# First experts' tiles of a two-layer transformer: each pair of adapter merges ahead of a tile instead of behind it

## The chip, the cores and the metric

The program runs on one core of one Trainium2 chip. The time is device microseconds of one execution; the profile is one further execution of the same program. Engines are named as in the profile: PE is the matrix engine (PEld its weight loads), DVE the vector engine, ACT the scalar engine, POOL the GpSimd engine, and SP the engine that issues most of the transfers.

## The reference, cut to what matters

Four sublayers on 8 batches of 512 tokens with 512 features, each followed by a residual sum and a layer norm: a causal attention with 16 heads, a mixture of 8 experts, a second attention, and a quantised feed-forward layer. The mixture is the one that the change touches:

```python
router_logits = xf @ gate_weight.T + xf @ gate_delta.T
probs = softmax(router_logits)
routing_weights, selected = top_k(probs, 2)
gup = einsum('th,eho->teo', xf, gate_up_proj)
gup = gup + 2.0 * einsum('ter,eor->teo', einsum('th,erh->ter', xf, gup_lora_A), gup_lora_B)
gates, h = split(gup, 2)
h = silu(gates) * h
out = einsum('tei,eih->teh', h, down_proj)
out = out + 2.0 * einsum('ter,ehr->teh', einsum('tei,eri->ter', h, down_lora_A), down_lora_B)
y = sum over the two selected experts of out * routing_weights
x = layernorm(x + y)
```

Each expert has low-rank adapters of rank 16 for both of its matrices. The adapters' product depends on no token, so it can be added to the weights once.

## The kernel before

Only the two selected experts of a token are computed. A routing step writes each token into a table by expert, rows are gathered by that table into tiles of 128 tokens of one expert, and each tile goes through that expert's three products. The work on the first attention, the routing, the merging of adapters and the first tiles lies in one function, `attention0`. The order of PE's instructions there is the order in which the Python code makes them (`in_order(tc)`, entered at L1481); the orders of DVE, ACT, POOL and SP are made by a scheduler, which also picks the buffer that a tile of a pool gets.

**A tile** (`Tiles.step`, L938) puts on PE, in this order: half of the gate and up product of the next tile (two matmuls of 128x512 at L903), the two transposes of this tile's hidden rows (L911), the other half (L903), the product with the down matrix (two matmuls at L919), and four transposes that turn the rows of the tile three further on (L878). ACT and DVE make the activation (L904, L905), copy the transposed rows (L913, L879) and the result (L192 or L194); SP stores the result (L928), POOL issues the gather of a later tile's rows (L842). These have PSUM buffers of their own.

**A merge** (`merge`, L1404, which calls `Experts.merge`, L786) adds one of six slices of the adapters of a pair of experts to their weights. It makes two matmuls (L781), one for each expert of the pair; each has 16 rows and 512 columns, and the two lie in different groups of the array's rows. Each result stands in a buffer of the PSUM pool `a_mm` (tag `mm`), which has **two buffers** in all. ACT copies each out with a factor of 2 (L792, tile `scaled`), and POOL adds the copy to the weights (L794).

**Routing** shares those two buffers: the transposes of a batch's rows (`turn`, L1320, four buffers one after another), the router's logits (`score`, L491), their way back to tokens (`choose`, L503, read by DVE at L510 and L511), the ranks of tokens within experts (`dispatch`, L547 and L548, read by DVE at L554), one-hot rows made by DVE alone (`one_hot`, L577 to L579), and the table (`enter`, L588, sixteen matmuls of 128x256 in bf16, read by DVE at L589 and L590).

At the end of `attention0`, when the last batch's attention is done, the order is written out by hand. Of the 24 merges, 14 have been made by then. What follows alternates routing of the last two batches, tiles and merges: the table of the last batch but one (`enter`), two tiles each followed by a merge, `turn` of the last batch, a tile, `score`, a merge, `choose`, a tile, a merge, `dispatch`, two rounds of `one_hot`, tile and merge, the table of the last batch, and then tile and merge until no merge is left. These tiles are all of experts 0 to 3, while the merges are of experts 4 to 7. The result of a merge is wanted only by tiles behind this stretch.

The routing of the last batch is not wanted by these tiles either: their rows come from batches 0 to 5 (`t_soon`). Tiles further on take rows by the finished table (`t_fixed`).

Of the kernel before, what the change touches and what calls it, by code (L numbers as in the profile page):

```python
# [1213 lines left out]
def attention0(env, guard, keep, routes, experts, dram, p_mm, tiles_ctx):  # L1214
# [8 lines left out]
    with ExitStack() as phase:  # L1223
# [55 lines left out]
        def mm(shape, name):  # L1279
            return p_mm.tile(shape, F32, tag="mm", name=name)  # L1280
# [51 lines left out]
        def choose(b):  # L1332
            router.choose(b, logits.pop(b), mm([P, NT, E], "ps_r"))

        def dispatch(b):
            router.dispatch(b, mm([P, NT, E], "ps_rank"))
# [3 lines left out]
        def one_hot(b, places):  # L1340
            if places[0] == 0:
                rooms[b] = work.tile([P, ND, S], F32, tag="x1T", name="one_hot")
            return router.one_hot(b, rooms[b], places)

        def enter(rows):
            router.enter(mm([P, 2, E * E_TILES], "ps_table"), *rows)
# [57 lines left out]
        def merge(n=1):  # L1404
            for _ in range(min(n, len(merges))):
                e, c = merges.pop(0)
                ps = [mm([P, 512], "ps_lora") for _ in range(2)]
                experts.merge(e, c, ps, [work.tile([P, 512], F32, tag="r_inv", name="scaled", bufs=2) for _ in ps])
# [100 lines left out]
        project(b, 3)  # L1509
        experts.load(7)  # L1510
        enter(rows)
        for _ in range(2):
            tiles.step()
            merge()
        for c in range(ND):
            turn(b, c)
        tiles.step()
        score(b)
        merge()
        choose(b)  # L1520
        tiles.step()
        merge()
        dispatch(b)
        for places in ((0, 1), (2, 3)):
            rows = one_hot(b, places)
            tiles.step()
            merge()
        enter(rows)
        tiles.of_fixed = router.fixed(routes)
        while merges:  # L1530
            tiles.step()
            merge()
        order.close()
    return router, tiles, router.tables(routes, p_mm.tile([P, E], F32, tag="mm", name="ps_count"), guard.routed[:, 1:2])

# [289 lines left out]
def usual_pass(tc, ins, held_out):  # L1825
    nc = tc.nc
    with ExitStack() as ctx:
# [4 lines left out]
        with tc.tile_pool(name="a_mm", bufs=2, space=PSUM) as p_mm, ExitStack() as attn1_ctx:  # L1832
            with tc.tile_pool(name="routes", bufs=1, side="right") as routes, \
                    tc.tile_pool(name="experts", bufs=1, side="right") as pool, ExitStack() as tiles_ctx:
                experts = Experts(env, pool)
                router, tiles, tables = attention0(env, guard, keep, routes, experts, dram, p_mm, tiles_ctx)

                def load_rows(b):
                    rows = router.rows[S * b : S * (b + 1)]
                    nc.sync.dma_start(out=env.xs[b], in_=rows.rearrange("(t p) d -> p t d", p=P))  # L1840

                env.open_stream(ctx, range(2))
                rows = ctx.enter_context(tc.tile_pool(name="c_rows", bufs=1))
                own = attn1_ctx.enter_context(tc.tile_pool(name="c_own", bufs=1))
                attention = Attention1(env, guard, router, rows, own, p_mm, dram)
                beside = {tiles.next + 6 * (b + 1): lambda b=b: load_rows(b) for b in range(2)}

                for i, piece in enumerate(attention.first_pieces()):
                    beside[E * NT + 4 + 2 * i] = piece
                with in_order(tc, mybir.EngineType.DVE, mybir.EngineType.Activation, mybir.EngineType.Pool,  # L1850
                              mybir.EngineType.SP):
                    while tiles.next < tiles.n:
                        tiles.step()
                        next(tables, None)
                        beside.pop(tiles.next, lambda: None)()
                assert not beside and next(tables, None) is None
                tiles.rare()
# [314 lines left out]
```

## Time and profile before

| | |
|---|---|
| time, median of 3 runs (lowest, highest) | 2221.11 us (2220.45, 2225.37) |
| time of the profiled execution | 2228.55 us |
| its span, first to last instruction | 2226.8 us |
| mean granted TensorE clock over the span | 0.993 |
| PE busy | 2191.9 us, 98% of the span |
| first and last of the ten merges that the change moves, start | 773.10 and 849.53 us |
| POOL's addition of one expert's slice (L794), 48 times | median 1272 ns |
| ACT's copy of one expert's slice (L792), 48 times | median 597 ns |

In rows of the timeline the first column is the start in us from the span's start and the second the time to the end of the last instruction that the row merges; `xN` is the count. One fp32 matmul shows as two records. A bracket at the end of a row holds the idle time of the engine just before it and what ended it. In rows of windows the columns are the stretch, busy time and number of instructions of PE, PEld, DVE, ACT and POOL, then the granted clock of TensorE (1.00 is full speed), the share of the DMA engines and GB/s.

### The profile page before, as it was taken

To read this page: it belongs to the slowest core of one execution; us is meant where nothing else is said; L and a number is where in the kernel's file an instruction comes from. 1 tells how busy PE (TensorE), PEld (TensorE's weight loads), DVE (VectorE), ACT (ScalarE), POOL (GpSimd) and SP (SyncE) were. 2 spreads that over 40 slices of the span, in tenths; PEclk is the share of its full clock that TensorE was granted. 3 is DMA by queue.
4 is the path that set the end of the run, shared out by engine and by line. 5 is a ranking of instruction groups with operands and counts; after the bars stand their busy time and mean duration, and the time that the engine had idled before them with its cause. 6 is when DMAs were issued, how large, how long until landed. Compare 5 with 4: busy or idle time off the path is not lost. (4 is left out here: it accounts for less than half of the span.)

```text
span 2226.8 us, 23678 instructions
## 1 busy us (share of the span) xinstructions
PE 2191.9 (98%) x9006; PEld 1116.6 (50%) x9006; DVE 1273.7 (57%) x2032; ACT 632.0 (28%) x917; POOL 487.6 (22%) x489
## 2 busy tenths in 40 slices
PE   9999999999999999999999999999999999999997
PEld 3344444444444444444443333333343778888876
DVE  3556666666666633323316887798757655555443
ACT  2332323323233232122124333223332222222222
POOL 2322423234132333122105222222211000000000
PEclk9999999999999899999999999999999999999999
DMA  8010101101022216888735212312110321111000
GB/s 297 20 57 1 57 10 48 58 1 58 5 71 94 85 57 181 227 218 214 191 114 193 80 57 86 95 55 77 45 32 13 109 78 57 57 57 57 20 20 21
DMA packets 146428, 182.20 MB, mean 82 GB/s; under 512 B 60530, under 2 KB 89202, under 8 KB 144514
## 3 DMA queue, kind: packets, MB, share of 16 engines
q1 hardware_dynamic: 135024, 144.91, 21.0%
q0 software_dynamic: 10560, 34.61, 5.5%
q8 instruction: 74, 1.21, 0.2%
q10 hardware_dynamic: 722, 1.07, 0.1%
q14 instruction: 48, 0.39, 0.1%
HBM read 117.38 MB, written 63.18 MB: 81 GB/s over the span
## 5 line engine op out<-in xcount | busy, mean ns | idle before, releaser
L903 PE MATMUL ps_gu<-experts,xrT 128*128 128x512 f32 (+1 forms) x520 | 248.8, 601 | 0.0
L1360 ACT ACTIVATE p<-sc 128x2048 f32<-128x2048 f32 (+1 forms) x96 | 152.8, 1592 | 190.0 <-PE sc L1356 183.1
L1148 DVE SCALAR_TENSOR_TENSOR hT<-ps_u,vec,sg 128x512 f32<-128x512 f32 x88 | 65.6, 745 | 195.2 <-PE ps_u L1143 195.2
L1365 POOL TENSOR_SCALAR_AFFINE_SELECT p<-p 128x512 f32<-128x512 f32 x128 | 91.6, 729 | 385.2 <-ACT p L1360 378.5
L1159 PE MATMUL ps_f<-ffn_w,h_half 128*128 128x512 f32 x672 | 170.2, 394 | 0.6 <-issue 0.4
L998 POOL TENSOR_TENSOR g_total<-g_total,r_inv 128x512 f32<-128x512 f32 x64 | 89.7, 1401 | 358.3 <-DVE r_inv L1735 283.0
L1705 ACT ACTIVATE p<-sc 128x1024 f32<-128x1024 f32 x128 | 124.0, 1021 | 105.9 <-PE sc L1702 100.8
L1735 DVE RECIPROCAL r_inv<-r_inv 128x512 f32<-128x512 f32 x32 | 107.1, 3346 | 78.8 <-ACT r_inv L995 78.8
L1388 DVE TENSOR_TENSOR p<-p 128x1536 f32<-128x1536 f32 (+2 forms) x96 | 129.4, 1348 | 39.2 <-POOL p L1365 22.2
L905 DVE TENSOR_TENSOR h<-ps_gu,h 128x256 f32<-128x256 f32 x67 | 28.4, 424 | 212.8 <-ACT h L904 212.8
L903 PEld LDWEIGHTS ps_gu<-experts,xrT 128*128 128x128 f32 x520 | 96.2, 197 | 89.7 <-issue 89.5
L1159 PEld LDWEIGHTS ps_f<-ffn_w,h_half 128*128 128x128 f32 x672 | 124.4, 188 | 33.0 <-DVE h_half L1154 5.6
L1143 PE MATMUL ps_g<-x_high,ffn_w 128*128 128x512 f32 x352 | 138.9, 395 | 0.8 <-DVE x L1676 0.8
L1143 PE MATMUL ps_g<-x_low,ffn_w 128*128 128x512 f32 x352 | 139.1, 395 | 0.0
L1143 PE MATMUL ps_u<-x_low,ffn_w 128*128 128x512 f32 x352 | 138.8, 394 | 0.0
L1143 PE MATMUL ps_u<-x_high,ffn_w 128*128 128x512 f32 x352 | 138.7, 394 | 0.0
L919 PE MATMUL ps_y<-experts,hT 128*128 128x512 f32 (+1 forms) x272 | 127.9, 593 | 0.5 <-ACT hT L913 0.5
L1702 PE MATMUL sc<-qT,kT 64*128 64x512 f32 x512 | 127.3, 615 | 1.0 <-ACT qT L1609 0.7
L1292 PE MATMUL ps_q<-experts 128*128 128x512 f32 x256 | 121.1, 615 | 4.4 <-DMA experts<-in_xT 4.4
L1724 PE MATMUL av<-p,v 128*64 128x512 f32 x512 | 123.8, 605 | 0.0
L1285 PE MATMUL ps_v<-experts 128*128 128x512 f32 x256 | 118.0, 609 | 3.3 <-DVE v L1287 3.3
L1670 PE MATMUL ps_o<-attn_out,aoT 128*128 128x512 f32 x256 | 117.9, 605 | 0.8 <-ACT r_inv L995 0.8
(262 smaller groups left out, 3438.5 us busy)
## 6 DMA issues: line engine op xcount, KB each, us to landing
results<-y SPq DMA_DIRECT2D x68, 256.0 KB, 2.3
turned<-turned SPq DMA_DIRECT2D x56, 256.0 KB, 4.1
pair<-xrT SPq DMA_DIRECT2D x25, 512.0 KB, 3.4
xrT<-pair SPq DMA_DIRECT2D x100, 128.0 KB, 4.5
x<-in_x SPq DMA_DIRECT2D x8, 1024.0 KB, 7.5
experts<-in_gate_up SPq DMA_DIRECT2D x8, 1024.0 KB, 10.8
rows<-x SPq DMA_DIRECT2D x32, 256.0 KB, 2.0
x<-rows SPq DMA_DIRECT2D x8, 1024.0 KB, 15.5
```

The source lines that it names most:

```text
L903: nc.tensor.matmul(ps, lhsT=xT[:, c, :], rhs=self.weights(i, c), start=c == 0, stop=c == ND - 1)
L919: self.nc.tensor.matmul(ps, lhsT=hT[:, c, :], rhs=self.weights(i, ND + c), start=c == 0, stop=c == self.NI - 1)
L1143: nc.tensor.matmul(ps, lhsT=w[:, ts(dc, P)], rhs=x[:, dc, :], start=(dc, i) == (0, 0), stop=(dc, i) == (ND - 1, 1))
L1159: self.nc.tensor.matmul(os[t], lhsT=h[:, ts(t, P)], rhs=self.weights(2 * NHID + c), start=(c, i) == (0, 0), stop=(c, i) == (NHID - 1, 1))
L1285: nc.tensor.matmul(ps, lhsT=xts[b][:, c, ts(t, P)], rhs=wv[:, c, :], start=c == 0, stop=c == ND - 1)
L1292: nc.tensor.matmul(ps, lhsT=wq[:, g, ts(c, P)], rhs=xts[b][:, c, :], start=c == 0, stop=c == ND - 1)
L1360: nc.scalar.activation(p, sc[:, :, :width], AF.Exp, scale=scale)
L1388: nc.vector.tensor_tensor(total[:, :, P * kt :], total[:, :, P * kt :], p[:, :, at : at + w], ALU.add)
L1670: nc.tensor.matmul(ps, lhsT=state[b]["aoT"][:, c, ts(t, P)], rhs=w_out[:, c, :], start=c == 0, stop=c == ND - 1)
L1702: nc.tensor.matmul(sc[:, j, :], lhsT=st["kT"][hs, ts(kt, P)], rhs=st["qT"][g][hs, :], start=True, stop=True)
L1705: nc.scalar.activation(p, sc, AF.Exp, scale=scale)
L1724: nc.tensor.matmul(st["av"][HD * j : HD * (j + 1), :], lhsT=st["v"][:, kt, HD * j : HD * (j + 1)], rhs=p[:, j, :], start=kt == 0, stop=kt ...
```

## The change

Every merge of the stretch that stood directly behind a tile is called directly ahead of it. The matmuls, copies and additions stay the same in number and size, and so do the tiles and the routing steps; what changes is what lies next to what. Seen from routing: the table of the last batch but one is now followed by a merge, then a tile; `turn`, `dispatch` and the last batch's table now follow a tile instead of a merge; `choose` and `dispatch` and that table are now followed by a merge; `score`, merge, `choose` and merge stand in one row.

```diff
         enter(rows)
+
         for _ in range(2):
+            merge()
             tiles.step()
-            merge()
         for c in range(ND):
             turn(b, c)
         tiles.step()
         score(b)
         merge()
         choose(b)
+        merge()
         tiles.step()
-        merge()
         dispatch(b)
         for places in ((0, 1), (2, 3)):
             rows = one_hot(b, places)
+            merge()
             tiles.step()
-            merge()
         enter(rows)
         tiles.of_fixed = router.fixed(routes)
         while merges:
+            merge()
             tiles.step()
-            merge()
         order.close()
```

In the program built from it the instructions of all engines are the same in kind and number. The buffers of `a_mm` that the scheduler picks, called 0 and 1 here, are these (before, then after), in PE's order from the first table on; a bar is a tile, and M is a merge's pair:

```
before  table 1 | M 0,1 | M 0,1  turn 0,1,0,1 | logits 0  M 1,0  r 1 | M 0,1  rank 0 | M 1,0 | M 1,0  table 1 | M 0,1 | M 0,1 | M 0,1 | M 0,1
after   table 1  M 0,0 | M 1,0 | turn 1,0,0,1 | logits 0  M 1,0  r 1  M 0,1 | rank 0  M 1,1 | M 0,1 | table 0  M 1,0 | M 1,0 | M 1,0 | M 1,0 |
```

Behind the stretch the buffers of `a_mm` alternate in both programs, with 0 and 1 exchanged.

## The prediction

> **What bounds the kernel now.** I read the page first, for the engine that is never idle:
>
> ```profile
> span 2226.8 us, 23678 instructions
> ...
> PE 2191.9 (98%) x9006; PEld 1116.6 (50%) x9006; DVE 1273.7 (57%) x2032; ACT 632.0 (28%) x917; POOL 487.6 (22%) x489
> ...
> PEclk9999999999999899999999999999999999999999
> ```
>
> PE is busy for 98% of the span, and no other engine for more than 57%. A microsecond that PE loses in the stretch of the change is therefore lost at the end as well, unless a later wait takes it up, and behind the stretch hardly any are left. The last row says that the granted clock dips in one slice of 55.7 us, the one from 779 us on, which is the stretch of the change. The second view is PE's waits from 760 to 852 us, all of them:
>
> ```profile
> PE ps_x1T L1320 <- ACT scaled L792: 0.7, 1, 0.7
> PE ps_rank L547 <- ACT scaled L792: 0.7, 1, 0.7
> PE ps_table L588 <- ACT scaled L792: 0.7, 1, 0.7
> PE ps_x1T L1320 <- DVE x1T L194: 0.3, 1, 0.3
> ```
>
> Each of the first three is a routing step that wants one of the two buffers of `a_mm` straight after a merge took both, so it waits until ACT has copied one out. These are the waits that a tile in between would hide. The third view is the timeline, here of a tile between two merges and of the `turn` behind the second, and, from earlier, of how long a buffer is held:
>
> ```profile
> 738.85 0.60 ACT L792 ACTIVATE scaled<-ps_lora 128x512 f32<-128x512 f32 x1 [2.16 <-PE ps_lora L781]
> 739.49 0.29 PEld L781 LDWEIGHTS ps_lora<-lora 16*128 16x128 f32 x2 [0.44 <-ACT scaled L792]
> ...
> 767.20 1.88 PE L903 MATMUL ps_gu<-experts,first_turned 128*128 128x512 f32 x4
> ...
> 773.10 1.13 PE L781 MATMUL ps_lora<-lora 16*128 16x512 f32 x4
> 774.16 1.98 PE L903 MATMUL ps_gu<-experts,xrT 128*128 128x512 f32 x4
> ...
> 780.16 1.13 PE L781 MATMUL ps_lora<-lora 16*128 16x512 f32 x4
> 782.03 1.15 PE L1320 MATMUL ps_x1T<-ident,x 128*128 128x128 f32 x8 [0.74 <-ACT scaled L792]
> ```
>
> A tile takes PE 5.90 us (767.20 to 773.10) and a merge's pair 1.06 us (773.10 to 774.16); its two matmuls lie in different rows of the array and run beside each other. The first two rows belong to two merges in a row: a matmul of a merge that began at 737.63 was copied from 738.85 to 739.45, and the next user of its buffer began at 739.49. **A buffer is held for 1.86 us from the matmul's start.** The last view is the granted clock in six stretches of 3.41 us, which is the step in which it changes:
>
> ```profile
> 781.29:784.70 3.41, 2.37 (x18) 1.96 (x18) 1.23 (x2) 1.77 (x4) 2.70 (x3) 1.00 0.49 156
> 791.53:794.94 3.41, 3.41 (x14) 1.74 (x14) 0.38 (x2) 2.72 (x4) 1.83 (x3) 1.00 0.44 141
> 794.94:798.36 3.42, 3.42 (x7) 1.60 (x6) 2.55 (x17) 1.35 (x4) 0.74 (x1) 0.50 0.00 0
> 801.77:805.18 3.41, 2.67 (x12) 1.36 (x12) 1.83 (x7) 1.08 (x2) 1.53 (x2) 1.00 0.21 77
> 805.18:808.60 3.42, 3.42 (x7) 1.38 (x6) 3.35 (x19) 0.37 (x1) 0.96 (x1) 0.50 0.00 0
> 818.84:822.25 3.41, 2.67 (x20) 1.77 (x20) 0.95 (x2) 1.08 (x2) 1.53 (x2) 1.00 0.20 77
> ```
>
> The clock is halved behind the second and the fourth of them, and not behind the first and the last. What tells them apart is how full the array was: time of streaming, times the share of its rows and columns in use. A merge's pair is four records of 0.43 us on 16 of 128 rows, 0.21 us. From 801.77 that is 0.21 for the merge, some 0.05 for the ranks and 1.09 of the tile from 804.09 on: 1.35 of 3.41, a fill of 0.40. From 791.53 it is 0.30. From 818.84 it is 0.21 for the merge and 1.53 of table, 0.51; from 781.29 it is 0.59. A fill of up to 0.40 was followed by half the clock, one of 0.51 was not. A tile that meets a halved window took 7.68 us (794.08 to 801.76, and 804.09 to 811.77 again), so a window costs 7.68 - 5.95 = 1.73 us; 5.95 lies between the tiles of 5.90 and, from 812.83, 6.00 us.
>
> **The change part by part.** Nothing is added or removed in number; what changes is which wait stands where. The buffers are those that the built program names.
>
> *`turn`* follows a tile. Before, merge, wait and transposes took 780.16 to 784.40, 4.24 us. The wait of 0.74 goes. But its third buffer is now that of the second chunk, which ACT copied out 1.77 us after the first transpose (783.21 + 0.59 against 782.03), where before the third began 1.44 us after it: transposes 2.37 + 0.38 = 2.75. With the merge, 1.06 + 2.75 = 3.81: **-0.43**.
>
> *The first table* is followed by a merge whose two matmuls both get buffer 0, since buffer 1 holds the table until DVE has read it, and DVE is then behind four layer-norm rows until 771.5. The second matmul waits for the copy of the first: 1.86, and then its own 0.86 (two records of 0.43), 2.72 us against 1.06: **+1.66**. At most it takes a pair's 1.06, and the term is 1.86. ACT has been idle there for 19 us, so the copy is not late. Behind the waiting matmul PE's whole queue stands.
>
> *`choose` and the merge behind it.* In the trace L503 gives way to the tile at 794.08. The first new matmul goes then; the second wants the buffer of `choose`, which DVE's L511 frees at 794.68, so it runs to 794.72 + 0.86 = 795.58: 1.50 against 1.06, **+0.44**. If DVE is late, this grows with it.
>
> *`dispatch`* loses its wait (801.76 to 803.62 was 1.86 for merge and wait; 1.06 remains, **-0.80**), but the merge behind it gets buffer 1 twice, **+1.66** as above.
>
> *The last table* loses its wait (818.83 to 820.70, 1.87; **-0.81**). The merge behind it uses both buffers, and the second is free when DVE has read the table: L590 ended at 823.52, 1.08 us after the table gave way at 822.44. So 1.08 + 0.04 + 0.86 = 1.98 against 1.06: **+0.92**. The remaining merges lie between tiles as before.
>
> What moves along costs nothing while its cover holds. POOL's additions (1.27 us each) stand in another order to the gathers (0.95 us), which serve a tile three further on, 17 us or more; SP's load of the next attention's weights (1536 KB, at 853.94) passes one result store, whose buffer is wanted again two tiles, 12 us, later. Without this cover each would cost its own length once.
>
> The sum without the clock: -0.43 + 1.66 + 0.44 - 0.80 + 1.66 - 0.81 + 0.92 = **+2.64 us**.
>
> *The clock.* The steps of 3.41 us lie at random to the program. One falls to 0.40 or less when it holds at most 1.37 us of work, so some 1.15 of tile beside a merge and 2.25 of an almost empty stretch. A stretch of length L then catches one with a chance of about (L - 1.1)/3.41. Before: merge, wait and `choose` (791.30 to 794.08, 2.8) 0.5, merge and ranks (2.33) 0.36; the profiled execution had both. After: table's merge (2.72) 0.48; both merges around `choose` (791.30 to 795.58, 4.3) 0.94; ranks and merge (0.47 + 2.72 = 3.2) 0.62. That is 2.0 against 0.86, and a halved window makes the rest of an empty stretch longer, so that a second follows more easily. I take **two more windows, +3.46**, between one (1.73) and three (5.19).
>
> The Trainium skill, page "TensorE: Matmul & The Clock Gate", section "Why this matters for your kernels", asks only that no idle gap between bursts be longer than about 3 us. The longest gap that I add is 1.0 us, so by that rule no window is added and the sum is +2.6 us. The rows above speak against it: the window from 791.53, after which the clock is halved, has PE busy in all its 3.41 us.
>
> **The sum.** +2.64 + 3.46 = +6.1 us. The profiled execution took 2228.55 us, 7.4 more than the median of the runs, with the clock halved in seven steps of 3.41 us up to 810 us; on it the sum gives 2234.7, and on the median, which I forecast, **2227.2 us**.
>
> **The rivals.**
>
> *No more halved windows (2223.8 us).* Only the +2.64 remain. For it: the first of the three new places catches a window only every other time. Against it: the stretch around `choose` is longer than a step. 0.22.
>
> *The windows vanish (2220.3, not slower).* The place is `dispatch` and `choose`: a tile now lies between the merge and the ranks, and if both windows of before go and none comes, 2.64 - 3.46 = -0.8. It decides where every empty stretch is under 2.25 us; the doubled buffers speak against it. 0.06.
>
> *The change does what it says (2218.9, not slower).* The three waits go, -2.2, and the doubled buffers cost nothing because the second matmul could go elsewhere. The built program speaks against it. 0.07.
>
> *DVE is held up by POOL (2229.7).* The merge behind `choose` brings two additions of 1.27 us beside DVE's chain of small steps (795.46 to 799.40). At 804.40 and 805.22 two steps of 0.18 us took 0.56 and 0.97, while POOL added. The ranks wait for the chain; PE comes to them at about 801.5, so the chain has 2 us of cover, and what exceeds it, at most the 2.5 us of both additions, is added to my sum. 0.13.
>
> **How the numbers follow.** My forecast has 0.52, with 2225.5 to 2228.9 as its own range (one to three windows). A measurement here tells 0.2%, 4.4 us, from no change, so "slower" begins at 2225.55. It takes nearly all of the forecast (0.48), the last rival (0.13) and the upper edge of the first (0.04): 0.65. "Faster" needs less than 2216.7, 0.02. The rest, 0.33, is no change. The range goes from 2222.5, below the first rival by one window's share of the runs' spread, to 2231.5, the last rival with another window.
>
> **What would show it.** Right: PE's waits name `scaled` in front of L781 twice, about 1.0 us each, none of the three old waits is left, and the granted clock is halved three to five times between 763 and 825 us. Wrong: both matmuls of the merges behind the first table and behind the ranks start together, or the halved steps there stay at two or fewer. If the ranks wait for DVE, the last rival has its place.

## The result, and the profile after

| | before | after |
|---|---|---|
| time, median (lowest to highest; runs) | 2223.61 us (2220.45 to 2226.35; 8) | 2231.10 us (2227.98 to 2232.48; 8) |
| time of the profiled execution | 2228.55 us | 2231.41 us |
| its span | 2226.8 us | 2229.6 us |

The ratio of after to before is 1.0036, with a 95% interval of 1.0026 to 1.0045: the changed kernel is 7.5 us slower. The forecast was 2227.2 us, +6.1 us on a median of 2221.11. The direction was right and the time lies in the range of 2222.5 to 2231.5, but the size is off by 3.9 us.

The three rows of the page of after that answer to those of before:

```profile
span 2229.6 us, 23679 instructions
...
PE 2194.0 (98%) x9006; PEld 1116.6 (50%) x9006; DVE 1278.5 (57%) x2032; ACT 633.2 (28%) x917; POOL 488.5 (22%) x489
...
PEclk9999999999999899999999999999999999999999
```

PE still bounds everything. These totals hardly show the loss, since a matmul at half the clock counts as busy. Nor does the last row: its one dip, here the slice from 724.6 to 780.4 us, comes from four halved steps between 722 and 746 us, ahead of the stretch, and before has four there too. PE's waits in after, from 760 to 870 us, all of them:

```profile
PE ps_lora L781 <- ACT scaled L792: 1.5, 2, 0.7
PE ps_x1T L1320 <- ACT x1T L192: 0.7, 1, 0.7
```

The three waits of 0.7 us on `scaled` in front of `turn`, the ranks and the table are gone, as the change has it. In their place stand two of the same length in front of a merge's second matmul, where both matmuls of a merge got the same buffer (a doubled buffer, in what follows), and one inside the transposes. No wait on DVE is left or added. In the timeline of after:

```profile
765.51 1.12 PE L781 MATMUL ps_lora<-lora 16*128 16x512 f32 x2
767.38 1.12 PE L781 MATMUL ps_lora<-lora 16*128 16x512 f32 x2 [0.75 <-ACT scaled L792]
768.43 1.98 PE L903 MATMUL ps_gu<-experts,first_turned 128*128 128x512 f32 x4
...
781.40 1.04 PE L1320 MATMUL ps_x1T<-ident,x 128*128 128x128 f32 x8
783.12 1.09 PE L1320 MATMUL ps_x1T<-ident,x 128*128 128x128 f32 x8 [0.68 <-ACT x1T L192]
784.05 1.88 PE L903 MATMUL ps_gu<-experts,xrT 128*128 128x512 f32 x4
...
824.25 2.17 PE L781 MATMUL ps_lora<-lora 16*128 16x512 f32 x4
826.35 1.99 PE L903 MATMUL ps_gu<-experts,xrT 128*128 128x512 f32 x4
```

The first merge is torn apart, into two rows of two records: the second matmul begins 1.87 us after the first, and the tile begins 2.92 us after the merge, where a pair takes 1.06. The transposes take 784.05 - 781.40 = 2.65 us. The merge behind the last table takes 826.35 - 824.25 = 2.10. Then the granted clock in after, in some of the steps of 3.41 us in which it changes:

```profile
766.50:769.91 3.41, 2.66 (x7) 1.06 (x7) 2.91 (x4) 1.20 (x2) 2.38 (x3) 1.00 0.73 276
...
790.40:793.81 3.41, 3.41 (x21) 1.56 (x13) 0.35 (x1) 2.04 (x4) 1.81 (x2) 1.00 0.48 154
793.81:797.22 3.41, 3.41 (x6) 1.48 (x6) 2.25 (x10) 2.45 (x4) 2.09 (x3) 0.50 0.02 5
797.22:800.63 3.41, 3.41 (x7) 1.52 (x6) 3.24 (x13) 0.00 (x0) 1.91 (x2) 0.50 0.00 0
804.05:807.46 3.41, 2.66 (x13) 1.36 (x11) 3.25 (x13) 0.60 (x1) 0.70 (x1) 1.00 0.21 77
807.46:810.87 3.41, 3.41 (x5) 1.26 (x5) 3.38 (x12) 0.60 (x1) 1.83 (x2) 0.50 0.00 0
```

Three steps are at half the clock, two behind `score`, merge, `choose` and merge, and one behind the ranks and their merge. PE is busy in all of 790.40 to 793.81, and the clock is halved all the same; from 766.50, where it is idle for 0.75 us, it is not.

To compare executions I take the stretch from the first table's first matmul (L588) to `ps_count` (L623), which holds the same work in both kernels. In the profiled execution of before it took 91.05 us with two halved steps, in that of after 95.59 with three.

### The profile page after: what moved, and what is told of

It is laid out like the page before. It is cut to its first block, busy times and chain, and to the rows that moved or that the text cites. A ratio compares the mean times of both kernels' runs of the same rounds, so it can differ in the third digit from the quotient of the medians.

```text
span 2229.6 us, 23679 instructions
## 1 busy us (share of the span) xinstructions
PE 2194.0 (98%) x9006; PEld 1116.6 (50%) x9006; DVE 1278.5 (57%) x2032; ACT 633.2 (28%) x917; POOL 488.5 (22%) x489
```

## The experiments

The theory after the result: the loss has two parts, the merges whose second matmul waits for the copy of the first, and halved clock steps, which follow a step in which the array had too little work. By this theory the number of halved steps differs from execution to execution, since the steps of 3.41 us lie at random to the program, and that is also where before's own scatter comes from. The rivals: that idle time, not little work, brings the half clock; and that the clock plays no part in the difference at all.

**Both kernels again.** Neither is edited; each gives another profile.

> The kernel before once more, for its own number of halved clock steps. Theory: an execution's time is a base of 2216.4 us (2228.55 less seven halved steps of 1.73 us each) plus 1.73 us for each halved step that falls ahead of 850 us, and an execution at the median (2223.6) has about four of them; so this profile lies on that line within 1 us, and the two or three that the first profile had in the stretch from 763 to 850 us need not be there. Rival: the first profile lay 5 us above the median for another reason; then a profile near 2224 us shows seven halved steps as well.

> The changed kernel once more. Theory: base 2219.3 us (2231.41 less seven halved steps of 1.73), 2.9 us above the base of before, and three to five halved steps in the stretch from 763 to 850 us; the profile lies on that line within 1 us, the ratio to before is 1.003 to 1.0045. Rival (the loss is in the waits alone, the clock plays no part in the difference): as many halved steps as before's second profile in the stretch, and a time that does not follow their number.

Measured: 2224.91 us for before (11 runs, ratio 1.0004, 0.9993 to 1.0014) and 2231.27 us for after (7 runs, ratio 1.0033, 1.0021 to 1.0044). The stretch of each, as windows, first before and then after:

```profile
762.23:849.90 87.67, 85.15 (x308) 41.11 (x306) 34.03 (x102) 26.98 (x54) 35.96 (x32) 1.00 0.28 93
```

```profile
765.12:862.77 97.65, 95.48 (x307) 44.79 (x306) 37.08 (x102) 27.34 (x54) 36.08 (x32) 0.93 0.28 97
```

In this execution of before the stretch has no halved step and takes 3.38 us less than in the first, which had two: **1.69 us for a halved step**. The execution of after has four. The line that was expected of whole executions, a base and 1.73 us for each halved step, was a rough one: before's second lies 1.5 us below the 2216.4 + 4 x 1.73 that it should have had, after's second 0.2 below its own.

**A third profile of each**, to see whether the stretch keeps to a line.

> The kernel before, a third profile. Theory: from the first table's start to ps_count 87.67 us + 1.7 us for each halved step there (none, one or two), within 0.3 us. Rival (something else than the clock varies between executions): more than 0.5 us off that line.

> The changed kernel, a third profile. Theory: from the first table's start to ps_count 87.67 + 2.9 = 90.6 us + 1.7 us for each halved step there, of which there are two to four, within 0.5 us. Rival (something else than the clock varies between executions): more than 1 us off that line.

Measured: before 764.00 to 855.05, 91.05 us with two halved steps, the same to the hundredth as the first. After 763.30 to 860.92, 97.62 us with four, on its line within 0.3 us. In before nothing but the clock varies in the stretch; in after the three profiles, less 1.69 us for each halved step, agree to 0.4 us.

**Fuller matmuls.** This one tells the rivals apart: the same waits and buffers, but more of the array in use. It is a probe of time only: the five merges that it widens do not compute the product of one expert's adapters.

> As the changed kernel, but the matmuls of five merges, those next to routing, use all 128 rows of the array instead of 16, with zeros between the adapters; the product then holds the adapters of four experts and not of one. Where the second matmul of a merge waits for the copy of the first, this costs nothing (the first runs 0.86 of the 1.86 us either way); around score and choose some 0.5 us in all. Waits and buffers stay. Theory (a step of 3.41 us is followed by half the clock when the array was filled to 0.40 or less): the stretch from 763 to 850 us has no halved step or one, and the time is 2231.1 - 4 x 1.73 + 0.5 = about 2224.7 (2222.5 to 2227.5). Rival (the waits, that is PE's idle time, bring the half clock): three to five halved steps as in the changed kernel and 2231 to 2232. Rival (the clock plays no part in the difference): 2231 to 2232 too, whatever the number of halved steps.

```diff
+        i and self.nc.gpsimd.memset(self.lora, 0.0)
...
-    def delta(self, ps, e, c):
+    def delta(self, ps, e, c, wide):
         j = 32 * (e % 4)
-        a, bt = lora_factors(self.lora[j : j + R, :], c)
+        a, bt = lora_factors(self.lora if wide else self.lora[j : j + R, :], c)
...
-                experts.merge(e, c, ps, [...])
+                experts.merge(e, c, ps, [...], len(merges) in (9, 7, 6, 5, 3))
```

Measured: 2225.57 us (11 runs, ratio to before 1.0005, 0.9996 to 1.0015), 5.7 us less than the changed kernel in the same series. Its waits of PE are the very two rows shown for after. Its merge behind the ranks, and its clock in the steps around `choose` and the ranks and over the stretch:

```profile
800.51 1.10 PE L781 MATMUL ps_lora<-lora 128*128 128x512 f32 x2
802.36 1.13 PE L781 MATMUL ps_lora<-lora 128*128 128x512 f32 x2 [0.75 <-ACT scaled L792]
803.32 1.88 PE L903 MATMUL ps_gu<-experts,xrT 128*128 128x512 f32 x4
```

```profile
789.79:793.20 3.41, 3.41 (x18) 1.82 (x14) 0.38 (x2) 2.54 (x4) 1.80 (x3) 1.00 0.48 154
793.20:796.62 3.42, 3.42 (x11) 1.69 (x10) 2.45 (x6) 1.99 (x5) 3.03 (x3) 1.00 0.02 5
800.03:803.45 3.42, 2.67 (x12) 1.37 (x11) 3.39 (x13) 0.60 (x1) 1.06 (x1) 1.00 0.20 77
803.45:806.86 3.41, 3.41 (x11) 1.57 (x10) 3.38 (x14) 0.97 (x2) 1.46 (x2) 1.00 0.00 0
...
762.86:852.85 89.99, 87.70 (x308) 42.75 (x307) 36.73 (x102) 27.29 (x54) 36.47 (x32) 1.00 0.30 105
```

No step is halved, though PE is busy for the same 2.67 of 3.42 us around the ranks as it was in after (2.66 of 3.41), where half the clock followed. The share of the array that works, counted as in the last section, is 0.60 in that step and was 0.19 in after. Idle time is the same, work is more: it is the work that counts. Both rivals, which wanted 2231 to 2232 us, fall.

**Parts of the change alone.** First the first loop alone, then `choose`'s merge alone, then all but the first loop.

> The kernel before with only the first loop's two merges ahead of their tiles. Buffers there are as in the changed kernel (both matmuls of the merge behind the table in buffer 0), everything behind the transposes as before. Theory (the doubled buffer costs 2.92 - 1.06 = +1.86 as seen in the changed kernel's profile, the transposes' wait gives -0.5, and the emptier stretch catches a halved step in some half of the executions, +0.8): before + 2.2 us, 2226.6 (2225.2 to 2228). Rival (merges lie as well here as there, the loss is around choose and the ranks alone): 2223.5 to 2224.5.

```diff
         for _ in range(2):
+            merge()
             tiles.step()
-            merge()
```

Measured: 2228.67 us (11 runs, ratio 1.0015, 1.0005 to 1.0025), +3.3 us by the ratio and 0.7 us above the range that I gave. The stretch takes 94.17 us with three halved steps, one of them new, at 767.76, behind the torn merge. Without them it is 1.43 us above before's; +1.86 for the merge and -0.5 for the transposes would be +1.36. The rival falls.

> The kernel before with only choose's merge ahead of its tile, so that score, merge, choose and merge stand in one row and the ranks follow a tile. Theory: +0.44 for the merge, -0.80 for the ranks' wait; the row of 4.3 us nearly always catches a halved step where before two places caught 0.3 of one each, +0.7: before + 0.3, 2224.7 (2223.5 to 2226); its profile shows one or two halved steps around choose and none at the ranks. Rival (DVE's chain is held up by POOL's two additions): the ranks wait for DVE and the time is over 2226.

```diff
         choose(b)
+        merge()
         tiles.step()
-        merge()
```

Measured: 2223.88 us (11 runs, ratio 1.0001, 0.9992 to 1.0010), no change that the runs can tell, and within the range that I gave. The stretch takes 89.04 us with one halved step, behind `choose`'s merge. In its waits of PE only the transposes and the table are left; the ranks wait for nobody:

```profile
PE ps_x1T L1320 <- ACT scaled L792: 0.7, 1, 0.7
PE ps_table L588 <- ACT scaled L792: 0.7, 1, 0.7
PE ps_x1T L1320 <- DVE x1T L194: 0.3, 1, 0.3
```

So POOL's two additions beside DVE's chain do not reach PE. Without its halved step the stretch is 87.35 us, 0.3 below before's: with -0.80 for the wait, +0.48 is left for the merge and the small steps around it.

> The changed kernel with the first loop's two merges back behind their tiles; the ranks' merge still has both matmuls in buffer 1. Theory: from the first table's start to ps_count, PE takes 87.67 us (the second profile of before, which had no halved step there) + 1.7 (0.4 for choose's merge, -0.8 and -0.8 for two waits, 1.86 and 1.04 for the merges behind the ranks and the last table) = 89.4 us, and 1.7 us more for each halved step, of which one to three are expected; the time is before + 4 us (2226.5 to 2229.5), and this gain over the changed kernel, 3 us, is what first_table lost. Rival (the two halves are not additive, since a halved step in the first half moves the phase of the second): over 2230, or under 2226.

```diff
         for _ in range(2):
-            merge()
             tiles.step()
+            merge()
```

Measured: 2228.87 us (12 runs, ratio 1.0020, 1.0011 to 1.0029); the stretch takes 94.18 us with three halved steps, 89.11 without them, where 89.4 was expected. The excesses add up, as far as intervals of 0.1% either way can tell: 0.15% for the first loop and 0.20% for the rest, against 0.33 to 0.36% for the whole.

**Merges inside tiles.** A merge directly ahead of a routing step made that step wait (before); one directly behind the first table or the ranks got a doubled buffer (after). Two versions put merges elsewhere.

> Merges neither behind a tile nor ahead of it but inside, between the tile's gate and up product and its product with the down matrix, so that no merge's buffer is wanted by the next routing step and no merge directly follows one. The merge between score and choose stays. Theory: the three waits of before go (-2.3 us), no merge waits for a copy, and the almost empty stretches are shorter than the 2.25 us that a halved step needs, but for score, merge and choose: at most one or two halved steps in the stretch. 2223.6 - 2.3 - 1.7 = about 2219.6 (2217.5 to 2221.5), faster than both kernels. Rival (the change's loss is not from where merges lie but from the tiles that come later): no better than before, 2223 to 2226. Rival (a merge inside a tile holds up the tile's own chain on ACT): waits of PE for hT or for ps_y's copy appear and the time is over 2224.

```diff
-    def step(self):
+    def step(self, middle=lambda: None):
...
+        middle()
         self.down(i)
...
-            tiles.step()
-            merge()
+            tiles.step(merge)
...
```

The same is done at all four places where a merge stood behind a tile. Measured: 2221.91 us (11 runs, ratio to before 0.9989, 0.9980 to 0.9998), 0.4 us outside the range that I gave. The expectation had missed one thing: the buffers of the transposes become 0, 1, 1, 0, and so one wait of 0.7 us on ACT's own copy stays. It is the only wait of PE in the stretch, which takes 88.01 us with one halved step, behind `score`, merge and `choose`.

> As the kernel with merges inside tiles, but one tile of the first loop goes between score and choose, and the tile behind the transposes takes a merge too: no routing step has a merge or another routing step beside it. Theory: the three waits and the 0.81 us between score's merge and choose go, -2.4 to -3.1, and no almost empty stretch is longer than 1.1 us, so no halved step falls between 763 and 850 us in its profile: before - 2.6 - 1.0 = 2220.8 (2218.8 to 2222), faster than both kernels and than the one with merges inside tiles by about 1 us. Rival (routing steps want tiles behind them for DVE's sake, and moving the transposes one tile forward makes them wait for the layer norm): PE waits for x at the transposes and the time is 2223 or more.

```diff
         enter(rows)
-        for _ in range(2):
-            tiles.step(merge)
+        tiles.step(merge)
         for c in range(ND):
             turn(b, c)
-        tiles.step()
+        tiles.step(merge)
         score(b)
-        merge()
+        tiles.step(merge)
         choose(b)
         tiles.step(merge)
```

The diff is against the version before it. Measured: 2220.58 us (11 runs, 2217.89 to 2222.47; ratio to before 0.9984, 0.9975 to 0.9993), as expected and **faster than both kernels**, before by 0.16%. The rival would have had the transposes wait for the layer norm; PE's waits are one row, on DVE's copy of an earlier chunk. That row, and the stretch:

```profile
PE ps_x1T L1321 <- DVE x1T L194: 0.5, 1, 0.5
```

```profile
763.52:849.06 85.54, 85.03 (x307) 40.10 (x306) 32.99 (x102) 26.98 (x54) 36.15 (x32) 1.00 0.28 98
```

**All profiled executions together.** The halved steps are those within the stretch; "full clock" is the stretch less 1.69 us for each; "outside" is the execution's time less the stretch.

| execution | time | stretch | halved | full clock | outside |
|---|---|---|---|---|---|
| before, first | 2228.55 | 91.05 | 2 | 87.67 | 2137.5 |
| before, second | 2221.80 | 87.67 | 0 | 87.67 | 2134.1 |
| before, third | 2226.92 | 91.05 | 2 | 87.67 | 2135.9 |
| after, first | 2231.41 | 95.59 | 3 | 90.52 | 2135.8 |
| after, second | 2234.64 | 97.65 | 4 | 90.89 | 2137.0 |
| after, third | 2232.63 | 97.62 | 4 | 90.86 | 2135.0 |
| fuller matmuls | 2224.59 | 89.99 | 0 | 89.99 | 2134.6 |
| first loop alone | 2228.97 | 94.17 | 3 | 89.10 | 2134.8 |
| `choose`'s merge alone | 2226.80 | 89.04 | 1 | 87.35 | 2137.8 |
| all but the first loop | 2227.31 | 94.18 | 3 | 89.11 | 2133.1 |
| merges inside tiles | 2224.02 | 88.01 | 1 | 86.32 | 2136.0 |
| and routing steps apart | 2221.11 | 85.54 | 0 | 85.54 | 2135.6 |

Outside the stretch the two kernels take the same: 2135.8 us on the mean of three executions of before, 2135.9 of after. Inside they take 89.92 and 96.95 on the mean, **7.03 us apart, of which 3.09 us are at the full clock and 3.94 us are 2.33 more halved steps**. The listed mean clocks of all runs say the same: a halved step of 3.413 us takes 1.707 us off the clock's full time, so (1 - clock) x time / 1.707 us is the number of halved steps in the whole program, and it is 6.6 on the mean over 73 runs of before and 9.0 over 15 of after, 2.4 more. (In every profile the last 6 to 9 us of the program, some 2.4 steps, are at half the clock and count here too.) It is 5.1 over the 11 runs of fuller matmuls and 5.3 over the 11 of the last version, so that the two profiles without a halved step in the stretch were hardly luck of where the steps fell.

## Why the prediction was right in kind and wrong in size

*Right: the mechanism, and where the loss sits.* The two waits in front of L781 stand where the prediction put them, behind the first table and behind the ranks, and all three old waits are gone. It asked for waits of about 1.0 us; the idle time is 0.75, since the row ahead of the wait lasts 1.12 us and not 0.86.

*The terms at the full clock*, forecast +2.64, measured +3.09:

| term | forecast | measured | from |
|---|---|---|---|
| `turn` | -0.43 | -0.53 | 1.06 + 2.65 against 4.24 |
| merge behind the first table | +1.66 | +1.86 | 2.92 - 1.06 |
| merge behind `choose` | +0.44 | +0.48 | `choose`'s merge alone |
| waits of ranks and last table | -1.61 | -1.61 | gone |
| merge behind the ranks | +1.66 | +1.86 | second profile of after, 808.35 to 811.26 |
| merge behind the last table | +0.92 | +1.04 | 2.10 - 1.06 |

The sum of the right column is 3.10. The step that was short is "the second matmul waits for the copy of the first: 1.86, and then its own 0.86". What follows the wait is 1.05 us long, as long as a whole pair, and that is the upper end that the prediction named and did not take. The 0.2 us go, in whole or in part, with the change between matmuls of 16 rows and of 128: with 128 rows throughout the same merge behind the first table took 2.73 us (764.61 to 767.34), and behind the ranks 2.81.

*The clock*, forecast two more halved steps at 1.73 us, +3.46; measured 2.33 at 1.69, +3.94. The chances for each place were somewhat low, as far as three profiles of each kernel tell: in the three profiles of after the first table's merge was caught twice, `choose` and the ranks three times each, 8 catches or 2.7 an execution against 0.48 + 0.94 + 0.62 = 2.0; in those of before both places were caught twice, 1.3 against 0.86. What lifts 8 catches to 11 steps is that one catch can halve two steps, which the prediction put down as "a second follows more easily".

*Wrong: the base.* This is the step that failed. The two parts sum to +6.1 us in the forecast and +7.0 in the profiles. What is left of the miss lies in the sentence "on the median, which I forecast, 2227.2 us": the sum was set on 2221.11 us, the median of three runs. The same kernel had 2223.61 in the eight runs beside the changed kernel, those three among them, and 73 later runs lie between 2219.16 and 2229.58 about a median of 2224.3. Of the 3.9 us between forecast and result, 2.5 are the base, 0.9 the two parts, and 0.5 lies within the scatter of runs. The prediction held the means to see this: it gave before 0.86 halved places in the stretch, noted that the profiled execution had two and lay 7.4 us above the median, and still took the lower figure for the kernel's own time. By its own numbers, 2228.55 less (2 - 0.86) x 1.73 is 2226.6 us. That the three runs came out low was chance; to build on them was not. That the time lies in the stated range is in part luck as well: it is above the forecast's own range, 2225.5 to 2228.9, and the range reaches so far only for the rival in which POOL holds up DVE, which did not happen.

*The profiled executions.* The prediction put 2234.7 us on the first profiled execution, and that of after took 2231.41, 2.86 us more than before's. Both have seven halved steps ahead of 870 us, before two in the stretch and five elsewhere, after three and four: the pair shows hardly more than the part at the full clock.

*A reading that was off by a slice.* The dip in the last row of the page of before stands for 723.7 to 779.4 us, not for the slice from 779 us on, and its four halved steps (from 723.26 and 740.33) lie ahead of the stretch. The two halved steps of the stretch show only in the rows of 3.41 us, and the sum rests on those.

*The rivals.* That no more halved steps come: fallen, by the count. That the steps vanish: fallen; they vanished only where the work was spread (the last version) or made fuller. That the change does what it says: fallen, by the two waits. That DVE is held up by POOL: in after two steps of DVE's chain are slowed, but PE's waits name no DVE, and `choose`'s merge alone cost nothing.

*The page's rule.* The Trainium skill, "TensorE: Matmul & The Clock Gate", "Why this matters for your kernels", asks that gaps between bursts of matmuls stay under about 3 us. In the stretch of after no gap of PE was longer than 0.75 us, and three to four steps were halved. The measurement decides: the rule is not enough here. The same page's section "What's actually happening" says that the window runs free of the kernel's start; the scatter above, none to two halved steps in one stretch of one kernel, agrees.

## What to carry to other kernels

Small matmuls on a few rows, short routing products and waits belong between full tiles one at a time: a step of 3.41 us in which the array had little to do was followed here by one that cost 1.7 us more, and two or three such things side by side were enough. Work that shares a pool of two output buffers goes into the middle of other work, away from the others that use the pool: on either side of a routing step a merge cost a wait here. Where the time of a kernel scatters by the clock, count the halved steps of the profiled execution before setting a forecast on a median of a few runs.

## What the runs showed of the hardware

**The clock follows the array's work.** I took each matmul record's streaming time (0.43 us for one of 512 fp32 columns at the full clock, twice that at half) times the share of rows and columns in use, over a step of 3.41 us, for all twelve profiles between 700 and 860 us. After a step at the full clock: up to a fill of 0.36 the next step was halved in 39 cases of 39, between 0.37 and 0.39 in two of five, from 0.41 on in none. After a halved step: up to 0.77 the next stayed halved (25 of 25), from 0.79 on it never did. At half the clock 0.78 is the work of 0.39 at the full clock, so one limit on work per step fits both. With the streaming time alone, or with the share of rows or of columns alone, no such limit comes out: some steps counted at 1.0 and more were followed by half the clock. That it is one limit on work explains double steps: at half the clock a step needs twice the time of full matmuls to get out.

**DVE beside POOL.** In after the merge behind the first table brings POOL's addition beside the layer norm, and the merge behind `choose` brings it beside the router's small steps. DVE in after:

```profile
767.00 3.82 DVE L185 TENSOR_SCALAR x<-x,mv,rstd 128x512 f32<-128x512 f32 x4 [1.49 <-POOL rstd L183]
...
796.66 1.29 DVE L522 TENSOR_TENSOR r_hots<-r_iota,red 128x32 f32<-128x32 f32 x1
797.99 1.19 DVE L527 SCALAR_TENSOR_TENSOR rest<-r_hots,pr 128x32 f32<-128x32 f32 x1
...
800.13 0.19 DVE L522 TENSOR_TENSOR r_hots<-r_iota,red 128x32 f32<-128x32 f32 x1
```

In before the four rows of L185 took 1.92 us, and L522 and L527 0.19 each. POOL's additions ran from 767.40 and 769.26 (1.27 us each) and from 796.64 to 799.13. PE did not wait for it here: the ranks, at 804.41, stand in no row of the waits. The Trainium skill, "SBUF — State Buffer", "Who interferes with whom", says that a DVE instruction with two inputs in SBUF contends with a GpSimd instruction that reads SBUF; L522 while POOL adds, 1.29 against 0.19 us, agrees.
